# Attributes and places carried in the factors' PSUM banks, the head's order, and VectorE's small steps, in a PaiNN block on one core

## Chip, core and metric

The kernel runs on one core of a Trainium2 chip. The metric is the device time of one execution in microseconds (us); the kernel before was run three times. Besides, one execution was taken by the hardware profiler; its page and its trace are what is read below.

Engines go by the profile's names: PE is TensorE (matrix products and transposes; PEld is its loading of weights), DVE is VectorE, ACT is ScalarE, POOL is GpSimd, SP is SyncE. PSUM is the memory into which PE writes: banks of 512 float32 columns on each of 128 lanes.

## What is computed

One message block of a graph network (PaiNN) with a residual and a layer norm, over 1250 nodes of 512 numbers (384 are three components of a vector of 128, by c and k; 128 are scalars `s`) and 40000 edges, sorted by destination. Cut to what matters here:

```python
x_j = x[src]                                   # 40000 x 512
v_j, s_j = x_j[:, :384].reshape(E, 128, 3), x_j[:, 384:]
s_j = silu(s_j @ W1 + b1) @ W3 + b3
rbf = sqrt(2 / R_CUT) * sin(n * pi * r / R_CUT) / r     # n = 1..20
edge_basis = rbf * cutoff(r) @ W2 + b2                  # 40000 x 384
s1, s2, s3 = split(s_j * edge_basis)
v_msg = v_j * s1[:, :, None] + s3[:, :, None] * edge_attr[:, None, :]
x = x + segment_sum(concat(v_msg, s2), dst)
# a second block on x: node products with U, V, Wu1, Wu2, gathered
# by src again and summed by dst; then layernorm(x_in + x)
```

## The kernel before

**Head.** The node part `silu(s W1 + b1) W3 + b3` is computed once a node, multiplied into the node's vectors, and stored as ten blocks of 128 rows of `table1` in DRAM (`make_rows`, `table_row`). Its inputs arrive over three DMA queues: SP's (`w1`, `b1`, `b3`, `w3`, destinations, sources, weights, later the attributes and the weights of the second part), ACT's and POOL's (node rows). `keep_warm(12)` lets PE multiply ones until there is work. Destinations (`dst_r`) become places in a window of 32 nodes (`local_r`, L346); two reductions and a product (L378) count the edges that miss their window, and a branch on that count picks the windowed form, the only one that runs here. `part_bias` splits bias rows into two half-precision parts, once for the first part's columns (DVE) and once for the second's (POOL). `by_tile` turns sources, weights and places so that an edge is a lane.

**Batches.** The edges are 20 groups of four chunks of 512. One batch takes 128 edges of each of the four chunks of a group, so there are 80 batches, t = 4g + i with i = 0 to 3. For batch t:

- `gather(t)` (L756, POOL): four indirect DMAs bring 128 rows of `table1` each, three batches ahead. The first of the four is made to wait for `edge_factors` of the batch that PE has just made.
- `edge_factors(t)` (L906, PE): four products of the turned basis (21 rows) with W2 and b2 give 384 columns of factors in each of the four banks of `eb`. Columns 384 to 511 of these banks are not used.
- `messages(t)` (DVE): L916 and L918 multiply the gathered rows by the factors, in place; then what is listed under `amid`; then for batch t (`make_pair`, L939) and for batch t + 1 (`make_hot`, L847, `make_spread`, L859) the one-hot matrices of the edges' places, the latter two out of `sh.local` and `sh.attr`, which are parts of `sh.carried` (places and three attributes for each edge) in SBUF.
- `add_messages(t - 1)` (L955, L961, PE) sums the messages of the batch before into `agg` by the one-hot matrices.
- `count_links(t - 1)` (L976 at a group's first batch, L984; PE) counts weighted links between nodes into the bank `adj`, for the second block. It uses 400 columns of `adj`. The rest hold a table of halves (L802) and, copied on ACT every fourth group by `bring_fades` (L809), the fades of four groups, which DVE reads in `make_basis` and `make_turns`.
- `distances(t + 1)` (L871) and `mark_sources(t + 1)` (L881) make the one-hot matrices of sources on ACT, four operations each.

Every other group needs a new basis: `make_turns` in four parts (three on DVE, part 3 is a sine on ACT), `make_basis` for each of two groups (L814, DVE), and `turn_basis` (four transposes on PE, L823, and a copy on ACT, L828). At the end of a group, `close_group` on ACT copies the sums (L1000, L1006) and, in `close_links` (L1019 to L1024), the counts' high parts; `low_counts` (L1030, DVE) makes the low parts. For each block of 128 nodes the second part's node work follows on all engines (L1046 and on, L1092 among it).

**The order** is written out by hand. The main loop goes over t; in each step come `messages(t)`, the list `first`, `add_messages(t - 1)`, `count_links(t - 1)`, the list `early`, `edge_factors(t + 1)`, `gather(t + 3)`, and the lists `mid`, `late` and `dve`. Each list is sorted by rank. Every engine has a queue of its own and works in this order; waits between engines follow from the data. In a step that has something under `amid`, except a group's first, `count_links` comes behind `edge_factors` and `gather`:

```python
behind = set(amid) - {last + 1 for last in last_step.values()}
...
    if 1 <= t <= NT:
        add_messages(t - 1)
        if t not in behind:
            count_links(t - 1)
    run(early, t)
    if t + 1 < NT - 2:
        made = edge_factors(t + 1)
    ...
    if t in behind:
        count_links(t - 1)
```

For g > 1 with an odd number (base = 4g - 4) `amid` holds `make_turns` part 0 in t = base - 3, `make_basis(g)` in base + 2 and `make_basis(g + 1)` in base + 4; and for every group `low_counts` in the second step of the group after. `turn_basis` is in `first` of base + 3 and in `early` of base + 5, rank 1. `mark_sources` has rank 5 in `early`.

## Time and profile before

| | |
|---|---|
| three runs, median (lowest, highest) | 571.47 us (568.67, 572.39) |
| the profiled execution, its own time | 567.24 us |
| its span in the profile | 565.4 us |
| mean granted clock of PE | 0.907 of full |
| busy: PE, DVE, ACT, POOL | 79%, 76%, 67%, 62% |
| indirect DMAs, software queue | 104.47 MB, 62.6% of 16 engines' span |

How to read the lines: in a timeline, a row is start in us, duration in us, engine, line of the kernel, operation, the tile written <- the tiles read, their shape and the number of instructions it groups, and in brackets the idle time of the engine before it with what ended that idle time. In the waits, a row is the waiting engine, tile and line <- what released it: microseconds of idle time, number of waits, the longest. On the page, a group's row ends with busy time and mean nanoseconds of one, then the idle time ahead of them and its main releaser. "issue" is idle time for which the profile shows no cause.

### The profile page before, as it was taken

How to read it: one execution, taken by the hardware profiler on the slowest of the kernel's cores; microseconds unless marked ns; L12 is line 12 of the kernel's file. 1: busy time of each engine (PE TensorE's matmuls, PEld its weight loads, DVE VectorE, ACT ScalarE, POOL GpSimd, SP SyncE). 2: the span in 40 equal slices, each digit the busy share in tenths (PEclk: the TensorE clock that was granted, in tenths of full speed). 3: DMA queues.
4: the chain of work that ended last, by engine and by line, in shares of the span. 5: the costliest groups of instructions: out<-in, count | busy, mean ns of one | idle time of the engine just before them, and what ended most of it. 6: DMA issues, size and time to landing. Idle time of an engine off the chain costs nothing.

```text
span 565.4 us, 11226 instructions
## 1 busy us (share of the span) xinstructions
PE 444.6 (79%) x4257; PEld 249.3 (44%) x4257; DVE 432.1 (76%) x660; ACT 377.0 (67%) x955; POOL 350.1 (62%) x377
## 2 busy tenths in 40 slices
PE   8557667677878787767887797879789698989993
PEld 6323233353344344435433443545445354445682
DVE  5576687778877877886778778787878887797675
ACT  3493565567777566775757687577768766788663
POOL 7775666666666666665556665666666666574530
PEclk9856998979897979988788897999989999999997
DMA  8786777777777776776777787678778777877413
GB/s 247 269 243 188 227 228 221 226 214 227 234 222 203 239 223 214 228 230 192 209 217 217 205 258 231 193 234 250 220 237 229 236 224 223 265 217 237 157 56 133
DMA packets 37938, 123.29 MB, mean 218 GB/s; under 512 B 7296, under 2 KB 9870, under 8 KB 37874
## 3 DMA queue, kind: packets, MB, share of 16 engines
q0 software_dynamic: 25824, 104.47, 62.6%
q1 hardware_dynamic: 10850, 17.35, 9.3%
q8 instruction: 35, 0.57, 0.4%
q10 hardware_dynamic: 1200, 0.66, 0.4%
q14 instruction: 29, 0.24, 0.2%
HBM read 112.94 MB, written 9.51 MB: 217 GB/s over the span
## 4 chain that ended last, share of the span: by engine, by line
PE 55%; DVE 20%; ACT 13%; issue 6%; another core or an unknown queue 3%; DMA 2%; POOL 0%; SPq 0%; DVEq 0%; POOLq 0%
PE eb L906 11%; PE agg L955 8%; PE agg L961 6%; DVE more L918 5%; PE adj L984 5%; PE begun L1359 5%; ACT one L881 5%; DVE nodes L918 4%; DVE more L916 3%; PE work L1146 3%; DVE nodes L916 3%; PE work L1051 2%; PE work L823 2%; ACT one L871 2%
## 5 line engine op out<-in xcount | busy, mean ns | idle before, releaser
L756 POOL DMA_INDIRECT more<-table,src_i x189 | 188.8, 999 | 106.2 <-issue 43.0
L756 POOL DMA_INDIRECT nodes<-table,src_i x124 | 123.5, 996 | 68.4 <-issue 28.6
L881 ACT ACTIVATE one<-one,weight,src_f 128x128 f16<-128x128 f16 x313 | 128.6, 483 | 0.2
L916 DVE TENSOR_TENSOR more<-more,eb 128x1024 f32<-128x1024 f32 (+2 forms) x48 | 57.2, 1193 | 63.8 <-PE eb L906 29.9
L871 ACT ACTIVATE one<-number,low 128x128 f16<-128x128 f16 x313 | 99.8, 393 | 6.9 <-remote 4.6
L906 PE MATMUL eb<-w_sb,basis_t 21*128 21x384 f32 x614 | 78.9, 577 | 29.4 <-DVE more L918 14.5
L918 DVE TENSOR_TENSOR more<-more,eb 128x1536 f32<-128x1536 f32 (+2 forms) x48 | 81.8, 1705 | 0.0
L916 DVE TENSOR_TENSOR nodes<-nodes,eb 128x1024 f32<-128x1024 f32 x30 | 36.6, 1222 | 39.4 <-PE eb L906 21.3
L955 PE MATMUL agg<-more,hot 128*32 128x512 f32 x378 | 61.7, 687 | 5.2 <-ACT sums L1006 5.2
L961 PEld LDWEIGHTS agg<-more,spread 128*32 128x32 f32 x1134 | 39.6, 119 | 37.8 <-issue 36.6
L984 PE MATMUL adj<-pair,one 128*128 128x160 f16 x313 | 38.0, 243 | 22.6 <-DVE basis L814 18.7
L918 DVE TENSOR_TENSOR nodes<-nodes,eb 128x1536 f32<-128x1536 f32 x30 | 52.4, 1747 | 0.0
L961 PE MATMUL agg<-more,spread 128*32 128x128 f32 x1134 | 48.6, 291 | 2.7 <-issue 2.7
L906 PEld LDWEIGHTS eb<-w_sb,basis_t 21*128 21x128 f32 x614 | 26.5, 198 | 51.9 <-issue 22.8
L859 DVE TENSOR_TENSOR spread<-hot,carried 128x384 f32<-128x384 f32 (+1 forms) x81 | 44.4, 549 | 2.7
L955 PE MATMUL agg<-nodes,hot 128*32 128x512 f32 x248 | 40.6, 658 | 3.9 <-ACT sums L1006 3.8
L984 PEld LDWEIGHTS <-one 128*128 128x128 f16 x313 | 23.4, 103 | 38.3 <-issue 36.4
L939 DVE TENSOR_TENSOR pair<-number,column 128x640 f16<-128x640 f16 (+1 forms) x81 | 38.7, 479 | 0.0
L961 PEld LDWEIGHTS agg<-nodes,spread 128*32 128x32 f32 x744 | 25.5, 118 | 23.1 <-issue 22.7
L961 PE MATMUL agg<-nodes,spread 128*32 128x128 f32 x744 | 31.8, 289 | 1.0 <-issue 0.9
L828 ACT COPY basis_t<-work 128x512 f32<-128x512 f32 x20 | 11.7, 587 | 29.6 <-PE adj L984 12.3
L1359 PE MATMUL begun<-upper,cast 128*128 128x512 f32 x57 | 28.1, 493 | 0.2 <-ACT cast L1350 0.2
(289 smaller groups left out, 711.2 us busy)
## 6 DMA issues: line engine op xcount, KB each, us to landing
table<-more SPq DMA_DIRECT2D x10, 320.0 KB
more<-table,src_i POOLq DMA_INDIRECT x189
spilled<-begun SPq DMA_DIRECT2D x10, 256.0 KB
more<-spilled SPq DMA_DIRECT2D x2, 1280.0 KB
node_x<-in_x_dram SPq DMA_DIRECT2D x35, 64.0 KB
nodes<-table,src_i POOLq DMA_INDIRECT x124
out_dram<-more SPq DMA_DIRECT2D x7, 256.0 KB
nodes<-in_x_dram POOLq DMA_DIRECT2D x2, 768.0 KB
```

The lines of the kernel that those rows point to most:

```text
L756: got = nc.gpsimd.indirect_dma_start(out=rows_t[:n, j, :], out_offset=None, in_=sh.table1, in_offset=bass.IndirectOffsetOnAxis(ap=sh.src_i ...
L859: nc.vector.tensor_mul(spread[t][:m, js], hots[t][:m, js, None, :].to_broadcast(shape), sh.attr[:m, g, e : e + n, :, None].to_broadcast(sh ...
L871: nc.scalar.activation(onehots[t][:, j, :], number[:, :P], AF.Abs, bias=low[:, e : e + 1])
L881: nc.scalar.activation(one, one, AF.Relu, scale=less[:, e : e + 1], bias=worth[:, e : e + 1])
L906: made = nc.tensor.matmul(made_in[t][:, j, :V], turned[g][rows, i, :], sh.w2_sb[rows, :], start=True, stop=True,)
L916: nc.vector.tensor_mul(msg[:m, js, V:], msg[:m, js, V:], factors_of(t, js)[:m, :, C:V])
L918: nc.vector.tensor_mul(msg[:m, js, :V].rearrange("p t (k c) -> p t k c", k=3), msg[:m, js, :V].rearrange("p t (k c) -> p t k c", k=3), fac ...
L939: nc.vector.tensor_tensor(pair[:m, js, :].rearrange("p t (l h) -> p t l h", h=2), number[:m, : PARTS * WIN].rearrange("p (l h) -> p l h", ...
L955: nc.tensor.matmul(agg[j * WIN : (j + 1) * WIN, :], hots[t][:, j, :], msg[:, j, :width], start=(i == 0), stop=False, skip_group_check=True,)
L961: nc.tensor.matmul(agg[j * WIN : (j + 1) * WIN, c * C : (c + 1) * C], spread[t][:, j, c, :], msg[:, j, width:], start=False, stop=(i == la ...
L984: nc.tensor.matmul(to[:, :, at : at + WIN], one[:m, j, :], pair[:m, j, :].rearrange("e (p n) -> e p n", n=WIN), start=(i == 0 and j == js[ ...
L1359: nc.tensor.matmul(acc, casts[a, b], rows[:, a, :], start=(start and a == first and k == 0), stop=(stop and a == end - 1 and k == 1),)
```

## The change

- **Carried columns.** A new step `bring_carried(g)`, for g = 1 to 18, copies the places and attributes of a group (16 tiles of 4 numbers, 64 columns) on ACT from `sh.carried` into columns 384 to 447 of bank 0 or 1 of `eb` (by g mod 2), in `early` of t = 4g - 3 at rank 6.5. `make_hot` and `make_spread` of those groups read them there.
- **The list `amid` is gone.** `low_counts` is at the end (`dve`) of a group's closing step t = 4g + 4; `make_turns` part 0 at the end of base - 3, part 3 at the end of base + 1; `make_basis(g)` and `make_basis(g + 1)` at the ends of base + 2 and base + 3. `count_links` is ahead of `edge_factors` in every step.
- **Head.** Half as many warming products; `w3` second on SP's queue; destinations ahead of the outer node rows there; fills of `dst_r` on DVE, of `src_r` later on POOL; the addition of MARGIN to the sources on DVE in place of POOL; the second bias rows and their `part_bias` earlier; three blocks of rows instead of one ahead of the product that counts the misses; eight loads of w2 and b2 from POOL's queue to SP's, behind the attributes.

```diff
--- before.py
+++ after.py
@@ -154,6 +154,8 @@
         return t
 
 
+    inside = SHARE * (NCP - 1) - MARGIN
+    assert all(0 <= inside - (SHARE * c - MARGIN) < WIN for c in range(full, NCP))
     ones = const.tile([P, P], F32)
     nc.vector.memset(ones, 1.0)
     warm = const.tile([P, 1], F32, name="warm")
@@ -164,23 +166,20 @@
         for _ in range(n):
             nc.tensor.matmul(idle[:, :P], ones, ones, start=True, stop=True)
 
-    keep_warm(12)
+    keep_warm(6)
     bias_f = front.tile([BIAS_ROWS - 1 + 32, V + 2 * C], F32, name="bias_f")
     nc.vector.memset(bias_f, 0.0)
+    dst_r = front.tile([NCP, CHUNK], I32, name="dst_r")
+    nc.vector.memset(dst_r[unfilled:, :], inside)
     sh.nodes = const.tile([P, NB * width], F32, name="nodes")
     sh.xt = sh.nodes.rearrange("p (b f) -> p b f", f=width)
     last = n_nodes + MARGIN - (NB - 1) * P
     nc.vector.memset(sh.xt[last // 32 * 32 :, NB - 1, :], 0.0)
     nc.vector.memset(sh.xt[:MARGIN, 0, :], 0.0)
 
-    inside = SHARE * (NCP - 1) - MARGIN
-    assert all(0 <= inside - (SHARE * c - MARGIN) < WIN for c in range(full, NCP))
-    dst_r = front.tile([NCP, CHUNK], I32, name="dst_r")
-    nc.gpsimd.memset(dst_r[unfilled:, :], inside)
     diff = front.tile([P, P], I32)
     nc.gpsimd.iota(diff, pattern=[[1, P]], base=0, channel_multiplier=-1)
     part = numbers([P, 1], [[0, 1]], 0, 1, "part")
-    nc.gpsimd.memset(sh.src_r[unfilled:, :], 0.0)
 
     size = CPG * (V + 2 * C)
     sh.more = const.tile([P, 3 * size], F32, name="more")
@@ -199,18 +198,19 @@
     of_s = slice(V, width)
     load_inner(nc.scalar, of_s, 1)
     sh.w1_sb = load(nc.sync, w1, [C, C], "w1_sb")
+    sh.w3_sb = load(nc.sync, w3, [C, V], "w3_sb")
     load_inner(nc.scalar, of_s, 5)
     nc.scalar.activation(warm, warm, AF.Silu)
     for b0 in (1, 5):
         load_inner(nc.gpsimd, slice(0, V), b0)
+    nc.gpsimd.memset(sh.src_r[unfilled:, :], 0.0)
     load_outer(nc.gpsimd, slice(0, V))
     sh.b1_sb = load(nc.sync, b1.rearrange("(p o) -> p o", o=1), [C, 1], "b1_sb")
     first_last = slice(0, 3, 2)
     three = bias_f.rearrange("(r q) f -> r q f", q=32)[:, 0, :]
     nc.sync.dma_start(three[:, :V], b3.rearrange("(o f) -> o f", o=1).to_broadcast([3, V]))
-    sh.w3_sb = load(nc.sync, w3, [C, V], "w3_sb")
+    load_edges(dst_r, dst)
     load_outer(nc.sync, of_s)
-    load_edges(dst_r, dst)
     load_edges(sh.src_r.bitcast(I32), src)
 
 
@@ -344,12 +344,6 @@
 
     local_r = front.tile([NCP, CHUNK], F32)
     nc.gpsimd.tensor_scalar(local_r, dst_r, share, None, op0=ALU.subtract)
-    nc.gpsimd.tensor_scalar(sh.src_r, sh.src_r.bitcast(I32), float(MARGIN), None, op0=ALU.add)
-    for i in range(GROUP):
-        nc.gpsimd.dma_start(w2_sb[i * FEAT : i * FEAT + N_RBF, :], w2)
-        nc.gpsimd.dma_start(
-            w2_sb[i * FEAT + N_RBF : i * FEAT + N_RBF + 1, :], b2.rearrange("(o f) -> o f", o=1)
-        )
     ends = front.tile([NCP, 2], F32)
     misses = front.tile([NCP, 1], F32)
     missed_i = fields.tile([1, 1], I32)
@@ -358,8 +352,15 @@
     make_rows((1, 2))
     inner_layer(next_s, (5, 6, 7, 8))
     load_edges(sh.wgt_r, edge_weight)
+    for h in range(2):
+        nc.sync.dma_start(
+            three[:, V + h * C : V + (h + 1) * C],
+            bu2.rearrange("(h o c) -> h o c", o=1, c=C)[2 * h].to_broadcast([3, C]),
+        )
+    part_bias(nc.gpsimd, slice(V, V + 2 * C))
     make_rows((3, 4))
     nc.vector.tensor_reduce(ends[:, 0:1], local_r, AX.X, ALU.min)
+    nc.vector.tensor_scalar(sh.src_r, sh.src_r.bitcast(I32), float(MARGIN), None, op0=ALU.add)
     rest_s = turn_s((0, 9))
     make_rows((5,))
     nc.vector.tensor_reduce(ends[:, 1:2], local_r, AX.X, ALU.max)
@@ -369,22 +370,20 @@
     nc.vector.scalar_tensor_tensor(
         misses, ends[:, 0:1], 0.0, ends[:, 1:2], op0=ALU.is_lt, op1=ALU.max
     )
-    for h in range(2):
-        nc.sync.dma_start(
-            three[:, V + h * C : V + (h + 1) * C],
-            bu2.rearrange("(h o c) -> h o c", o=1, c=C)[2 * h].to_broadcast([3, C]),
-        )
-    make_rows((7,))
+    make_rows((7, 8, 0))
     nc.tensor.matmul(missed, misses, ones[:NCP, 0:1], start=True, stop=True)
-    make_rows((8,))
     nc.vector.tensor_copy(missed_i, missed)
-    make_rows((0, 9))
+    make_rows((9,))
     by_tile(ps_front, sh.src_r, 0, 1, sh.src_f, 1)
     by_tile(ps_front, sh.wgt_r, 0, 1, sh.weight, 1)
     by_tile(ps_front, local_r, 0, 1, sh.local, 1)
     nc.vector.tensor_copy(sh.src_i, sh.src_f)
-    part_bias(nc.gpsimd, slice(V, V + 2 * C))
     load_edges(sh.att_r, edge_attr, 3)
+    for i in range(GROUP):
+        nc.sync.dma_start(w2_sb[i * FEAT : i * FEAT + N_RBF, :], w2)
+        nc.sync.dma_start(
+            w2_sb[i * FEAT + N_RBF : i * FEAT + N_RBF + 1, :], b2.rearrange("(o f) -> o f", o=1)
+        )
     sh.u_sb = load(nc.sync, u, [C, C], "u_sb")
     sh.v_sb = load(nc.sync, v, [C, C], "v_sb")
     sh.wu1_sb = load(nc.sync, wu1.rearrange("(h p) f -> p h f", p=C), [C, 2, C], "wu1_sb")
@@ -834,6 +833,18 @@
                 if m < P:
                     engine.memset(tile[m:, j], 0.0)
 
+        carried_at = {}
+
+        def bring_carried(g):
+
+            to = eb[:, g % 2, V : V + EPG * CARRY].rearrange("p (t k) -> p t k", k=CARRY)
+            nc.scalar.copy(to, sh.carried[:, g])
+            carried_at[g] = to
+
+        def carried_of(g):
+
+            return carried_at.get(g, sh.carried[:, g])
+
         def make_hot(t):
 
             g, i = batches[t]
@@ -847,7 +858,7 @@
                 nc.vector.tensor_tensor(
                     hots[t][:m, js, :],
                     lane[:m, None, :WIN].to_broadcast(shape),
-                    sh.local[:m, g, e : e + n, None].to_broadcast(shape),
+                    carried_of(g)[:m, e : e + n, 3:].to_broadcast(shape),
                     op=ALU.is_equal,
                 )
 
@@ -859,7 +870,7 @@
                 nc.vector.tensor_mul(
                     spread[t][:m, js],
                     hots[t][:m, js, None, :].to_broadcast(shape),
-                    sh.attr[:m, g, e : e + n, :, None].to_broadcast(shape),
+                    carried_of(g)[:m, e : e + n, :3, None].to_broadcast(shape),
                 )
 
         def distances(t):
@@ -920,7 +931,6 @@
                     msg[:m, js, :V].rearrange("p t (k c) -> p t k c", k=3),
                     factors_of(t, js)[:m, :, None, :C].to_broadcast([m, n, 3, C]),
                 )
-            run(amid, t)
             make_pair(t)
             if t == 0:
                 make_spread(0)
@@ -1448,7 +1458,7 @@
             last_step[g] = t
 
 
-        first, early, late, dve, mid, amid = {}, {}, {}, {}, {}, {}
+        first, early, late, dve, mid = {}, {}, {}, {}, {}
 
         def at(when, step, rank, fn, *args):
             when.setdefault(step, []).append((rank, fn, args))
@@ -1459,10 +1469,7 @@
             if g == NGR - 1:
                 at(dve, end - 4, 9, clear_unused, g)
                 at(early, end, 0.3, close_links, g)
-            if end + 1 < NT:
-                at(amid, end + 1, 1, low_counts, g)
-            else:
-                at(dve, end, 5, low_counts, g)
+            at(dve, end, 5, low_counts, g)
         for t in range(NT):
             if t + 1 < NT:
                 at(first, t, 9, distances, t + 1)
@@ -1470,17 +1477,14 @@
 
         for g in range(1, NGR, 2):
             base, n = 4 * g - 4, min(2, NGR - g)
-            if base:
-                at(amid, base - 3, 4, make_turns, g, n, 0)
-            else:
-                at(dve, 0, 4, make_turns, g, n, 0)
+            at(dve, max(0, base - 3), 4, make_turns, g, n, 0)
             at(dve, max(0, base - 2), 5, make_turns, g, n, 1)
             at(dve, base - 1 if base else 1, 6, make_turns, g, n, 2)
-            at(*((early, base + 1, 5.5) if base else (dve, 1, 7)), make_turns, g, n, 3)
-            at(amid, base + 2, 5, make_basis, g)
+            at(dve, base + 1, 7, make_turns, g, n, 3)
+            at(dve, base + 2, 5, make_basis, g)
             at(first, base + 3, 1, turn_basis, g)
             if n > 1:
-                at(amid, base + 4, 4, make_basis, g + 1)
+                at(dve, base + 3, 4, make_basis, g + 1)
                 at(early, base + 5, 1, turn_basis, g + 1)
 
 
@@ -1690,6 +1694,8 @@
         bring_fades(1)
         for g in range(1 + FADES, NGR, FADES):
             at(early, 4 * g - 3, 6, bring_fades, g)
+        for g in range(1, NGR - 1):
+            at(early, 4 * g - 3, 6.5, bring_carried, g)
         distances(0)
         mark_sources(0)
         ahead = 3
@@ -1697,7 +1703,6 @@
             gather(t)
         gather(ahead - 1, edge_factors(0))
         make_hot(0)
-        behind = set(amid) - {last + 1 for last in last_step.values()}
         for t in range(max(*first, *early, *late, *dve, *mid) + 1):
             if t < NT:
                 messages(t)
@@ -1710,8 +1715,7 @@
             run(first, t)
             if 1 <= t <= NT:
                 add_messages(t - 1)
-                if t not in behind:
-                    count_links(t - 1)
+                count_links(t - 1)
             run(early, t)
             if t + 1 < NT - 2:
                 made = edge_factors(t + 1)
@@ -1719,8 +1723,6 @@
                 edge_factors(t + 2)
             if t + ahead < NT:
                 gather(t + ahead, made if t + ahead < NT - 2 else None)
-            if t in behind:
-                count_links(t - 1)
             run(mid, t)
             run(late, t)
             run(dve, t)
```

## Prediction

> **What bounds the kernel now.** I read the page first. No engine is full over the span: PE 79%, VectorE (DVE) 76%, GpSimd (POOL) 62%, so the limit lies in a loop between engines.
>
> ```profile
> span 565.4 us, 11226 instructions
> PE 444.6 (79%) x4257; PEld 249.3 (44%) x4257; DVE 432.1 (76%) x660; ACT 377.0 (67%) x955; POOL 350.1 (62%) x377
> ...
> L756 POOL DMA_INDIRECT more<-table,src_i x189 | 188.8, 999 | 106.2 <-issue 43.0
> L756 POOL DMA_INDIRECT nodes<-table,src_i x124 | 123.5, 996 | 68.4 <-issue 28.6
> ```
>
> Next I read the timeline of one batch. It is t = 37, a batch with t mod 8 = 5 (t counts the 80 batches; t = 4g + i).
>
> ```profile
> 270.44 1.22 DVE L916 TENSOR_TENSOR more<-more,eb 128x1024 f32<-128x1024 f32 x1 [2.77 <-PE eb L906]
> 270.68 0.96 POOL L756 DMA_INDIRECT nodes<-table,src_i  x1 [2.17 <-PE eb L906]
> ...
> 271.58 1.75 DVE L918 TENSOR_TENSOR more<-more,eb 128x1536 f32<-128x1536 f32 x1
> ...
> 272.81 0.66 PE L823 MATMUL work<-ident,basis 128*128 128x128 f32 x4
> ...
> 273.39 0.93 PE L906 MATMUL eb<-w_sb,basis_t 21*128 21x384 f32 x8
> ...
> 274.47 1.22 POOL L756 DMA_INDIRECT nodes<-table,src_i  x1 [0.30 <-issue]
> ...
> 275.09 0.56 DVE L859 TENSOR_TENSOR spread<-hot,carried 128x384 f32<-128x384 f32 x1
> 276.43 0.59 ACT L828 COPY basis_t<-work 128x512 f32<-128x512 f32 x1 [3.14 <-PE adj L984]
> 276.52 1.22 DVE L916 TENSOR_TENSOR nodes<-nodes,eb 128x1024 f32<-128x1024 f32 x1 [0.87 <-PE adj L984]
> ...
> 276.91 1.65 ACT L881 ACTIVATE one<-one,weight,src_f 128x128 f16<-128x128 f16 x4
> ```
>
> Two things are to be seen. L906 starts 0.06 us after L918 ends (273.33) and is over at 274.32, yet L916 of the next batch begins only at 276.52. L823 is over at 273.47, and the scalar engine (ACT), idle for 3.14 us, takes its result only at 276.43. PE's results are seen by the others all at once, some 0.7 us after the end of the batch's fourth gather (274.47 + 1.22 = 275.69). In the last batches no gather runs, and the same product is seen 0.10 us after its end (519.95 + 0.92 = 520.87, then 520.97):
>
> ```profile
> 519.95 0.92 PE L906 MATMUL halves<-w_sb,basis_t 21*128 21x384 f32 x4 [0.18 <-DVE more L918]
> ...
> 520.97 0.68 DVE L916 TENSOR_TENSOR nodes<-nodes,halves 128x512 f32<-128x512 f32 x1
> ```
>
> So a batch is a loop: the signal of the factors releases L916 and the first gather (270.44, 270.68), four gathers follow, and then the next signal comes, 276.52 - 270.44 = 6.1 us later. I call the moment at which PE's results are seen "the late signal". It lies 3.2 us after L918's end. Whatever PE, ACT and DVE finish before it is hidden; what comes after it lengthens the batch.
>
> Last I read the waits between engines.
>
> ```profile
> PE adj L984 <- DVE basis L814: 18.7, 9, 2.7
> ...
> PEld adj L976 <- ACT adj L809: 10.0, 4, 3.2
> ...
> PE adj L976 <- ACT adj L809: 7.3, 4, 2.5
> ```
>
> These are the key to the change. L809 copies the fades into columns from 420 on of the bank `adj`; L976 writes columns below 400 of it, and waits for that copy in all four batches in which there is one. L814 reads the same spare columns, and L984 waits for it in nine batches. So a product waits for every earlier copy into, and read from, its bank, though the columns are others.
>
> **The change, part by part.** (A) *The copy `bring_carried`* is on ACT, in the early list at rank 6.5 of batch t = 4g - 3, g = 1 to 18, behind `mark_sources` (L881) and ahead of `edge_factors(t + 1)` (L906). It writes into a bank that L906 then writes, so by the waits above L906 must wait for it. In a batch with t mod 8 = 5, ACT's queue ahead of it is L828, which is released only by the late signal, and L881. From the rows: L828 at 276.43, L881 ends at 276.91 + 1.65 = 278.56. The copy has 64 columns a lane as L809 has, 0.20 us (row below): 278.76. L906 takes 0.93: 279.7. L916 starts then at 279.75 instead of 276.52, which is 3.2 us. The first gather of the next batch waits for the same product, so nothing of it is made up later. Nine batches (5, 13, ... 69): 9 x 3.2 = +29. Bounds: if L823's result reached ACT at once, with the links' 0.45 us (L984, ahead of L823 now) before it, L828 would start at 273.9, L881 end at 276.2, and the product at 277.35: 0.9 a batch, +8; if L881 is pushed too, 3.6, +32. I take 29, because L828 waited 3.14 here and the gathers stay as they are.
>
> (B) *Low counts ahead of the products*, with the copy of the batch after. `low_counts` (L1030) moves from behind the products of batch 4k + 1 to the end of batch 4k, where it needs L1024 of the same batch. This is t = 32 and 33:
>
> ```profile
> 242.86 1.22 DVE L916 TENSOR_TENSOR nodes<-nodes,eb 128x1024 f32<-128x1024 f32 x1 [1.40 <-PE work L1051]
> ...
> 243.46 0.56 ACT L1024 ACTIVATE counts<-high,shifts 128x320 f16<-128x320 f32 x1
> ...
> 245.66 0.48 DVE L1030 SCALAR_TENSOR_TENSOR counts<-counts,adj 128x320 f16<-128x320 f16 x1
> ...
> 247.37 1.63 ACT L881 ACTIVATE one<-one,weight,src_f 128x128 f16<-128x128 f16 x4
> ...
> 248.98 1.22 DVE L916 TENSOR_TENSOR nodes<-nodes,eb 128x1024 f32<-128x1024 f32 x1 [0.40 <-remote]
> 249.54 0.20 ACT L809 COPY adj<-fade 128x64 f32<-128x64 f32 x1
> 249.79 0.72 PE L976 MATMUL adj<-passed,ident 128*128 128x80 f32 x2 [2.54 <-ACT adj L809]
> ```
>
> L1024 ends at 244.02, L1030 would end at 244.5, and L916 of t = 33 starts there instead of at 242.86: 1.7 us. Behind it stand all of VectorE's products, and the pair, hot and spread of the next batch. Then L881 ends at 249.0, the fades (0.20) and the carried columns (0.20) follow, L906 ends at 250.35 and L916 of t = 34 starts at 250.4 instead of 248.98. The two delays overlap, so the pair of batches loses 1.4; another 0.4 if ACT's copy L1000, which came before the late signal here, comes with it. I take 1.6 for eight pairs (t mod 8 = 0 and 1): +13; bounds 0.8 (the copy finds its room) and 2.4: +6 to +19. At t mod 8 = 4 the same move is hidden by (A), at no cost; without that cover, about 0.9 in five batches.
>
> (C) *Waits that go.* With turns and basis at a batch's end, `count_links` stands ahead of L906 in every batch and neither L984 nor L976 waits for DVE or ACT there: 18.7 + 7.3 = 26 us of PE's idle time. Of this only what made L906 later than the late signal was on the path; a wait of 2 us is hidden by the 3.2. The worst case is the one above, 2.54 us at 249.79. I take a third: -8, bounds 0 and -26. The moved basis (L814) now needs L984's signal of its own batch and so follows the late signal by its 0.4; the next batch's loop (below) has 0.85 to spare, so it costs nothing; without that room, 18 x 0.4 = 7.
>
> (D) *Hot and spread read PSUM.* L906 then waits for the spread too. Pair, hot and spread take 0.40 + 0.32 + 0.56 = 1.3 behind L918 (274.37 to 275.65), so L906 runs from 1.3 to 2.3 instead of from 0.06 to 1.0 after L918. The late signal at 3.2 hides that: L916 to L918's end 2.9, 1.3, 0.93 and latencies are 5.2 of 6.1 us. Without this cover it is 1.3 for each of some 70 batches. The operations themselves: no row has a hot or a spread that reads PSUM. The nearest is L1092, as wide as a hot (128 columns) and with `work`, a PSUM bank, as an input: 0.28 against 0.29 of L847, which reads SBUF alone. I take 0 for both.
>
> ```profile
> 246.46 0.29 DVE L847 TENSOR_TENSOR hot<-lane,carried 128x128 f32<-128x128 f32 x1
> ...
> 247.83 0.28 DVE L1092 TENSOR_TENSOR x<-node_x,work 128x128 f32<-128x128 f32 x1
> ```
>
> The gathers may gain: 0.96 us is the undisturbed one (270.68), the mean of 313 is 0.998, together 12 us. I take nothing, as the signal in t = 37 came no later behind a gather of 1.22 than in other batches; bounds 0 and -12. The Trainium skill (GPSIMD Engine Reference, Key points) says that GpSimd shares its SBUF interfaces with VectorE and contends with its instructions of two SBUF inputs; hot and spread stop being such, while pair stays one. The stretched gather beside the spread at 274.47 agrees; by that page alone the sum would be up to 12 us less.
>
> (E) *Head.* Destinations load ahead of the outer rows, and the misses' product goes behind three more rows:
>
> ```profile
> 14.74 1.57 POOL L346 TENSOR_SCALAR local_r<-dst_r,share 80x512 f32<-80x512 int32 x1 [2.97 <-DMA dst_r<-in_dst_dram]
> ...
> 19.06 0.19 PE L378 MATMUL missed<-ones,misses 80*1 80x1 f32 x2 [2.07 <-DVE misses L369]
> ```
>
> PE's stop of 2.07 goes; adding MARGIN leaves POOL. Half of the warming products go as well. The w2 and b2 loads, eight issues, move past the attributes on SP's queue; they are needed only by the first L906. I take -2.5, bounds -4 and +1.
>
> Sum: 29 + 13 - 8 + 0 - 2.5 = +31.5. Against the profiled execution (567.24, span 565.4) that is 598.7. The three runs' median, 571.47, lies 4.2 above it, so the forecast of the median is 603.
>
> **Rivals.** *R1, the signal comes early:* PE's lateness belongs to the order in which L823 and L906 stand, not to the gathers, and ACT gets L823 at once. For it: L828's waits differ from batch to batch; against it: ACT idle at 276.43 with L823 done. Then (A) is +8: 571.5 + 8 + 13 - 8 - 2.5 = 582. *R2, the product is not held, and the kernel gets faster:* the factors' bank is guarded by columns. Then (A) is 0; in (B) the loop 2.9 + 0.1 + 0.93 has 2.1 to spare, more than 1.7, so 0; (C) and (E) stay: 571.5 - 10.5 = 561. It decides where L906 at t mod 8 = 5 starts within 0.1 us of L918's end. Against it: the four of four waits of L976 for L809. With the 12 us of the gathers it would be 549. *R3, it does not do what it says:* losses and gains of (B), (C) and (E) cancel and (A) is hidden, because ACT is ahead in the longer batches: 571.5 + 13 - 8 - 2.5 - 3 = 571. Against it: the late signal, not ACT's load, holds L828.
>
> **How the numbers follow.** Forecast 0.52, R1 0.18, R2 0.20, R3 0.10. R2 gets the most of the three, as its one condition, how the bank is guarded, decides the largest term, and the trace shows the guard only in another bank (`adj`). The likeliest is 603, with its own range 590 to 616 from the bounds of (A), (B) and (C). The range to be given reaches from 566, half way between R3 and R2, so that it leaves out R2 alone, to 616: 0.8. A measurement tells about 1% (5.7 us) from no change: slower 0.52 + 0.18 = 0.70, same 0.10, faster 0.20.
>
> **What would show it.** Right: in batches 5, 13, ... 69, L906 waits for the new copy, and the time from L916 to L916 is about 9.3 us instead of 6.1; in batches 1 mod 8, L916 waits for low counts; L984's wait for the basis is gone; the other batches stay at 6.0 to 6.1. Wrong: L906 starting at L918's end, no wait of PE for ACT's copy, or a batch of less than 6.0 us, which would mean that the late signal is not what sets the loop.

## The result and the profile after

The changed kernel takes 630.24 us (median of four runs, 629.89 to 631.30) against 571.93 us (four runs, 568.67 to 573.67) for the kernel before: ratio 1.103, 95% interval 1.098 to 1.108. The forecast was 603 with a range up to 616. The sign and the place of the largest loss were right, the size was not: 58 us were lost where 31.5 were forecast. Of the five terms of the sum only one, (A), came near what was measured.

The page after, its first lines and the groups of the gathers and of the factors' product (the product has line 917 now, the first multiplication of a batch 927, the copy of the carried columns 841):

```profile
span 628.5 us, 11273 instructions
PE 471.7 (75%) x4245; PEld 260.4 (41%) x4245; DVE 433.8 (69%) x662; ACT 378.2 (60%) x973; POOL 330.3 (53%) x367
...
L755 POOL DMA_INDIRECT more<-table,src_i x189 | 181.1, 958 | 152.6 <-PE eb L917 84.4
L755 POOL DMA_INDIRECT nodes<-table,src_i x124 | 117.9, 951 | 97.7 <-PE eb L917 54.1
L917 PE MATMUL eb<-w_sb,basis_t 21*128 21x384 f32 x614 | 83.5, 601 | 101.7 <-ACT eb L841 39.8
```

DVE and ACT are busy as long as before. POOL's gathers are shorter, 951 and 958 ns in place of 996 and 999, but its idle time ahead of them rose from 174.6 to 250.3 us (106.2 + 68.4 and 152.6 + 97.7), and its releaser is now the factors' product, which itself stood idle for 101.7 us, 39.8 of them for the new copy. PE is 27 us busier (471.7 against 444.6) with 12 instructions fewer: the same products run longer.

The batch t = 37 after (rows of the timeline: start, duration, what ended the idle time):

```profile
297.53 0.94 POOL L755 DMA_INDIRECT nodes<-table,src_i  x1 [0.30 <-issue]
297.54 1.21 DVE L927 TENSOR_TENSOR more<-more,eb 128x1024 f32<-128x1024 f32 x1
298.67 1.75 DVE L929 TENSOR_TENSOR more<-more,eb 128x1536 f32<-128x1536 f32 x1
...
299.10 1.94 PE L965 MATMUL agg<-more,hot 128*32 128x512 f32 x8
...
302.95 0.60 PE L822 MATMUL work<-ident,basis 128*128 128x128 f32 x4
...
303.59 0.59 ACT L827 COPY basis_t<-work 128x512 f32<-128x512 f32 x1 [2.35 <-PE work L822]
304.07 1.65 ACT L892 ACTIVATE one<-one,weight,src_f 128x128 f16<-128x128 f16 x4
305.62 0.20 ACT L841 COPY eb<-carried 128x64 f32<-128x64 f32 x1
...
305.88 1.61 PE L917 MATMUL eb<-w_sb,basis_t 21*128 21x384 f32 x8 [2.33 <-ACT eb L841]
...
307.77 0.94 POOL L755 DMA_INDIRECT more<-table,src_i  x1 [6.79 <-PE eb L917]
307.94 1.22 DVE L927 TENSOR_TENSOR nodes<-nodes,eb 128x1024 f32<-128x1024 f32 x1 [3.97 <-PE eb L917]
```

This is the chain that the prediction drew: turned basis, `mark_sources`, copy, product, and only then the next batch, 307.94 - 297.54 = 10.4 us after the last. One link differs: ACT takes the transposes (L822) as soon as they end, but they end late. Two of its durations are new: the product takes 1.61 in place of 0.93, and the sums L965 1.94 in place of 1.06 (both from t = 37 before).

Where the time went, by batch. The table adds, over the batches with the same t mod 8, the time from the start of one batch's first VectorE product (L916 or L927) to the next one's; it is worked out from the timelines. The columns are the profiled executions of five kernels, four of which are told of below.

| t mod 8 | before | after | c_early | no_carried | low_alone |
|---|---|---|---|---|---|
| 0 | 60.5 | 76.9 | 75.9 | 71.8 | 75.9 |
| 1 | 64.2 | 63.5 | 61.9 | 57.8 | 56.2 |
| 2 | 63.7 | 69.4 | 69.5 | 60.6 | 54.6 |
| 3 | 64.3 | 65.2 | 64.4 | 66.3 | 67.3 |
| 4 | 61.8 | 69.0 | 69.5 | 64.9 | 66.7 |
| 5 | 57.5 | 89.5 | 65.9 | 63.2 | 52.8 |
| 6 | 59.8 | 57.3 | 57.1 | 57.2 | 57.9 |
| 7 | 54.5 | 55.2 | 55.2 | 55.3 | 54.4 |

After against before: +32.0 in 5 mod 8, +16.4 in 0, +7.2 in 4, +5.7 in 2. Batches 2 and 4 mod 8, which were to stay at 6.0 to 6.1 us, take about 7.

### The profile page after: what moved, and what is told of

It is laid out like the page before. It is cut to its first block, busy times and chain, and to the rows that moved or that the text cites. A ratio compares the mean times of both kernels' runs of the same rounds, so it can differ in the third digit from the quotient of the medians.

```text
span 628.5 us, 11273 instructions
## 1 busy us (share of the span) xinstructions
PE 471.7 (75%) x4245; PEld 260.4 (41%) x4245; DVE 433.8 (69%) x662; ACT 378.2 (60%) x973; POOL 330.3 (53%) x367
## 4 chain that ended last, share of the span: by engine, by line
PE 53%; DVE 19%; ACT 16%; issue 7%; DMA 0%; another core or an unknown queue 0%; DVEq 0%; ACTq 0%
PE eb L917 15%; PE agg L965 10%; ACT one L892 6%; PE agg L971 6%; DVE more L929 5%; PE work L1156 3%; DVE more L927 3%; PE begun L1369 3%; DVE nodes L929 3%; PE adj L994 3%; DVE nodes L927 2%; ACT one L882 2%; PE work L1140 2%; DVE pair L949 2%; PE work L822 1%
## 5 line engine op out<-in xcount | busy, mean ns | idle before, releaser
L755 POOL DMA_INDIRECT more<-table,src_i x189 | 181.1, 958 | 152.6 <-PE eb L917 84.4
L755 POOL DMA_INDIRECT nodes<-table,src_i x124 | 117.9, 951 | 97.7 <-PE eb L917 54.1
L917 PE MATMUL eb<-w_sb,basis_t 21*128 21x384 f32 x614 | 83.5, 601 | 101.7 <-ACT eb L841 39.8
L927 DVE TENSOR_TENSOR more<-more,eb 128x1024 f32<-128x1024 f32 (+2 forms) x48 | 57.0, 1190 | 53.7 <-PE eb L917 36.3
L917 PEld LDWEIGHTS eb<-w_sb,basis_t 21*128 21x128 f32 x614 | 27.3, 200 | 125.1 <-ACT eb L841 43.9
L965 PE MATMUL agg<-more,hot 128*32 128x512 f32 x378 | 71.6, 821 | 2.5 <-ACT counts L1034 1.9
L971 PEld LDWEIGHTS agg<-more,spread 128*32 128x32 f32 x1134 | 44.1, 137 | 44.5 <-issue 42.7
L971 PE MATMUL agg<-more,spread 128*32 128x128 f32 x1134 | 52.7, 326 | 0.0
L927 DVE TENSOR_TENSOR nodes<-nodes,eb 128x1024 f32<-128x1024 f32 x30 | 36.5, 1217 | 23.0 <-PE eb L917 16.0
L1040 DVE SCALAR_TENSOR_TENSOR counts<-counts,adj 128x320 f16<-128x320 f16 x20 | 9.7, 487 | 47.7 <-ACT counts L1034 31.2
L965 PE MATMUL agg<-nodes,hot 128*32 128x512 f32 x248 | 40.7, 711 | 2.5 <-ACT sums L1016 1.3
L870 DVE TENSOR_TENSOR spread<-hot,eb 128x384 f32<-128x384 f32 x72 | 39.9, 554 | 2.5
L994 PE MATMUL adj<-pair,one 128*128 128x160 f16 x313 | 39.6, 253 | 1.0 <-issue 1.0
L949 DVE TENSOR_TENSOR pair<-number,column 128x640 f16<-128x640 f16 (+1 forms) x81 | 38.6, 477 | 0.0
L971 PEld LDWEIGHTS agg<-nodes,spread 128*32 128x32 f32 x744 | 27.1, 127 | 23.9 <-issue 23.4
```

Of the source, the lines that this page charges most:

```text
L755: got = nc.gpsimd.indirect_dma_start(out=rows_t[:n, j, :], out_offset=None, in_=sh.table1, in_offset=bass.IndirectOffsetOnAxis(ap=sh.src_i ...
L870: nc.vector.tensor_mul(spread[t][:m, js], hots[t][:m, js, None, :].to_broadcast(shape), carried_of(g)[:m, e : e + n, :3, None].to_broadcas ...
L917: made = nc.tensor.matmul(made_in[t][:, j, :V], turned[g][rows, i, :], sh.w2_sb[rows, :], start=True, stop=True,)
L927: nc.vector.tensor_mul(msg[:m, js, V:], msg[:m, js, V:], factors_of(t, js)[:m, :, C:V])
L949: nc.vector.tensor_tensor(pair[:m, js, :].rearrange("p t (l h) -> p t l h", h=2), number[:m, : PARTS * WIN].rearrange("p (l h) -> p l h", ...
L965: nc.tensor.matmul(agg[j * WIN : (j + 1) * WIN, :], hots[t][:, j, :], msg[:, j, :width], start=(i == 0), stop=False, skip_group_check=True,)
```

## The experiments

Runs told of together share a chip, and runs of the kernel before on it. They fell on five chips of two kinds: two on which the kernel before takes 567 to 573 us, as in the record above, and three on which it takes 494 to 496. Each run is therefore compared with the kernel before on its own chip, and times are subtracted only within one kind.

**The carried columns: alone, with the copy early, without, and in SBUF.** These four ran on one chip (before: 573.10 us). `c_alone` is the kernel before with the new step and the new reads of `make_hot` and `make_spread`. `c_early` is the changed kernel with one number changed:

```diff
-            at(early, 4 * g - 3, 6.5, bring_carried, g)
+            at(early, 4 * g - 3, 0.5, bring_carried, g)
```

`no_carried` leaves out the two lines that schedule the step, so that `carried_of` gives SBUF for every group. `sbuf_copy` keeps copy and rank, with another destination:

```diff
-            to = eb[:, g % 2, V : V + EPG * CARRY].rearrange("p (t k) -> p t k", k=CARRY)
+            to = pool.tile([P, EPG, CARRY], F32, name="brought", bufs=2)
```

> The kernel before with bring_carried alone (copy at rank 6.5, hot and spread read the factors' banks); nothing else of the change. Theory (the copy stands behind ACT's late work and holds the next product, since a product waits for an earlier copy into its bank): the nine batches with t mod 8 = 5 take about 9.3 us in place of 6.1, +29 to +32 in all, so 601 to 604 us. Rival (the loss of these batches comes from the other moves, low counts, turns and basis, and the copy only shows as the last releaser): below 580 us, batches 5 mod 8 at 6.1 to 6.8 us. If the shorter gathers (951 and 958 ns after, 996 and 999 before) come from hot and spread leaving SBUF, they are 950 to 960 ns here too.

> The changed kernel with the copy's rank 0.5 in place of 6.5: the same copy in the same batch, but on ACT ahead of the basis' copy and of mark_sources. Theory (it is the place in ACT's queue): batches 5 mod 8 fall from 9.9 us to 6.1 to 6.6, so 598 to 602 us. Rival (the product is held by hot and spread, which read its banks, whatever the copy does): L917 still waits, batches 5 mod 8 above 8 us, 620 us or more.

> The changed kernel without bring_carried: hot and spread read SBUF as before; all the other moves stay. Theory: batches 5 mod 8 at 6.1 us, -32 against the changed kernel: 596 to 600 us; gathers back at 996 to 999 ns mean. Second theory (reads of the factors' banks by hot and spread cost more, because they hold every product for 1.3 us): below 594 us, and below c_early by more than 4 us. Rival (the carried columns cost little): above 615 us.

> The changed kernel with the same copy at the same rank into an SBUF tile of its own, which hot and spread read. ACT does the same work in the same place; only the bank is not written and not read. Theory (the wait is on the bank): no product waits for this copy, batches 5 mod 8 at 6.1 to 6.6 us, 596 to 602 us. Rival (ACT's added work and its order are the cost, or hot waits for the late copy): batches 5 mod 8 above 8 us, 620 us or more.

Measured: `c_alone` 625.88 us (ratio 1.092, 1.084 to 1.100), `c_early` 602.95 (1.054, 1.046 to 1.062), `no_carried` 584.92 (1.022, 1.015 to 1.030), `sbuf_copy` 582.62 (1.015, 1.007 to 1.023). The columns alone cost 53 us, not 29 to 32; by the table's working 38.6 of them lie in batches 5 mod 8 and 14.7 in batches 1 mod 8, the two that have a copy. With the columns in, all other parts of the change add some 4 us. Moving the copy takes 27.3 us off the changed kernel; taking the columns away another 18.0; 11.8 are left. (The changed kernel's 630.24 is from the chip of the section above, where the kernel before takes 1.2 us less, so the 4 and the 27.3 are good to a us or two.) `sbuf_copy` does ACT's work in ACT's place without the bank and costs nothing beside `no_carried`, so the place in the factors' banks is the cost and not ACT's time. The theory of `c_early` (the place in ACT's queue, 598 to 602) came within 1 us. The first theory of `no_carried` (596 to 600) and that of `sbuf_copy` (596 to 602) missed by 11 us and more, since neither counted the reads. The second theory of `no_carried` (reads that hold the product) holds: 584.92 is below 594, and 18.0 below `c_early`.

The gathers did not follow their forecast: they take 964 and 966 ns in `c_alone`, but 972 and 959 in `no_carried`, where hot and spread read SBUF as before, and not 996 to 999. So what made them shorter is not only that hot and spread left SBUF, and stays open.

How the reads hold it: the waits of the product in `c_early` and in `no_carried` (waiting engine, tile, line <- releaser: us, times, longest).

```profile
PE eb L917 <- DVE spread L870: 23.5, 16, 2.4
...
PE eb L917 <- DVE hot L858: 11.2, 9, 1.6
PE eb L917 <- ACT eb L841: 10.8, 7, 1.9
```

```profile
PE eb L917 <- DVE more L929: 18.7, 14, 6.0
...
PE eb L917 <- DVE nodes L929: 11.1, 11, 2.2
```

What it costs is seen in t = 33, a batch behind a long one. First `no_carried`:

```profile
253.62 1.21 DVE L927 TENSOR_TENSOR nodes<-nodes,eb 128x1024 f32<-128x1024 f32 x1
...
256.81 0.93 PE L917 MATMUL eb<-w_sb,basis_t 21*128 21x384 f32 x8
...
258.49 1.26 POOL L755 DMA_INDIRECT more<-table,src_i  x1 [1.53 <-DVE x L1102]
...
258.85 1.21 DVE L927 TENSOR_TENSOR nodes<-nodes,eb 128x1024 f32<-128x1024 f32 x1
```

then `c_early`:

```profile
259.28 1.21 DVE L927 TENSOR_TENSOR nodes<-nodes,eb 128x1024 f32<-128x1024 f32 x1
...
262.79 0.55 DVE L870 TENSOR_TENSOR spread<-hot,eb 128x384 f32<-128x384 f32 x1
...
263.43 0.22 ACT L841 COPY eb<-carried 128x64 f32<-128x64 f32 x1 [1.14 <-DVE spread L870]
...
263.70 1.62 PE L917 MATMUL eb<-w_sb,basis_t 21*128 21x384 f32 x8 [1.83 <-ACT eb L841]
...
265.43 1.22 DVE L927 TENSOR_TENSOR nodes<-nodes,eb 128x1024 f32<-128x1024 f32 x1 [0.85 <-ACT adj L808]
265.61 0.94 POOL L755 DMA_INDIRECT more<-table,src_i  x1 [3.42 <-PE eb L917]
```

In `no_carried` the product starts 3.19 us after L927, and the batch takes 5.23. In `c_early` the copy waits for the spread, which reads its tile, and the product for the copy; it starts 4.42 us after L927, runs at the lower rate, and the first gather waits 3.42 us for it. The batch takes 6.15.

**The other three parts alone.** On one chip (before: 567.11 us, 25 runs), each on the kernel before. `low_alone`:

```diff
-            if end + 1 < NT:
-                at(amid, end + 1, 1, low_counts, g)
-            else:
-                at(dve, end, 5, low_counts, g)
+            at(dve, end, 5, low_counts, g)
```

`turns_alone` has the change's lines for `make_turns` and `make_basis` and nothing else of it; `head_alone` all lines of the change ahead of `windowed`; `before_again` is the kernel before, for its trace.

> The kernel before with low counts moved to the end of a group's last step, nothing else. Theory: batches 0 mod 8 take about 1.6 us more and batches 4 mod 8 0.5, those behind them somewhat less: 6 to 13 us more than before. Rival (what is lost in batches 0 mod 8 comes back in 1 mod 8, where low counts no longer stand ahead of pair, hot and spread): within 3 us of before.

> The kernel before with the turns and the basis moved to the ends of batches, nothing else. Theory (the links no longer wait for the basis, and hot and spread come earlier): 0 to 8 us less than before; on a chip with 495 us rather more, 5 to 15 us less, since low counts and copy made basis_back 17 us slower than the changed kernel there. Rival (keep_rest behind a basis that waits for PE): 3 to 8 us more, in batches 2 and 3 mod 8.

> The kernel before with the changed head, nothing else. Theory (w3 and the destinations ahead in SP's queue make the bias rows, and with them the table, late): the first product of the factors starts 0.9 us later or more, the first gather 1.4 us later or more; 1 to 6 us more than before. Rival (the forecast): 1 to 4 us less, first gather before 27.5 us.

> The kernel before unaltered, for its trace on this chip. Where it takes 570 to 575 us: batches at 6.0 to 6.1 us as in the trace of the forecast. Where it takes 490 to 500 us: theory (there PE's signals are seen at once, so the batch is set by DVE, ACT and the products and no longer by the fourth gather): L916 starts within 0.2 us of L906's end, or right behind DVE's own work, and most batches take 4.5 to 5.1 us. Rival (the gathers are quicker there): gathers at under 0.9 us each.

Measured: `low_alone` 567.51 us (0.999, 0.995 to 1.003), `turns_alone` 570.67 (1.003, 0.999 to 1.008), `head_alone` 569.00 (1.000, 0.996 to 1.004), `before_again` 565.82. None of the three can be told from no change. The theory of `low_alone` (6 to 13 us more) was too large, that of `turns_alone` (a gain) had the wrong sign, and that of `head_alone` (1 to 6 us more) is not borne out by the time, though its late start is: the first gather starts at 29.77 us, against 27.96 in `before_again` on the same chip. The rival was right for `low_alone`: the table has +15.4 in batches 0 mod 8, as forecast, and -8.0 and -9.1 in the two behind. Its timeline at t = 32 and 33:

```profile
235.38 1.22 DVE L916 TENSOR_TENSOR more<-more,eb 128x1024 f32<-128x1024 f32 x1 [1.14 <-remote]
...
238.32 0.93 PE L906 MATMUL eb<-w_sb,basis_t 21*128 21x384 f32 x8 [2.00 <-DVE more L918]
...
241.64 0.96 POOL L756 DMA_INDIRECT more<-table,src_i  x1 [1.28 <-PE work L1051]
242.00 0.56 ACT L1024 ACTIVATE counts<-high,shifts 128x320 f16<-128x320 f32 x1
...
242.59 0.49 DVE L1030 SCALAR_TENSOR_TENSOR counts<-counts,adj 128x320 f16<-128x320 f16 x1 [2.61 <-PE work L1051]
242.90 0.95 POOL L756 DMA_INDIRECT more<-table,src_i  x1 [0.30 <-issue]
243.00 1.21 DVE L916 TENSOR_TENSOR nodes<-nodes,eb 128x1024 f32<-128x1024 f32 x1
...
248.25 1.22 DVE L916 TENSOR_TENSOR nodes<-nodes,eb 128x1024 f32<-128x1024 f32 x1
```

DVE waits for ACT's counts (L1024, done at 242.56) and starts L916 1.6 us late, but the product was done, so POOL's first gather starts 1.36 us ahead of L916 (241.64 and 243.00) in place of 0.24 behind it. Its four gathers are over earlier, and the next batch takes 5.25 us. `turns_alone` was to gain; its batch 2 mod 8 shows why not (t = 34):

```profile
256.02 0.93 PE L906 MATMUL eb<-w_sb,basis_t 21*128 21x384 f32 x8
257.80 0.49 DVE L814 TENSOR_TENSOR basis<-turn,adj 128x320 f32<-128x320 f32 x1 [1.99 <-PE eb L906]
...
258.21 0.68 DVE L1097 TENSOR_TENSOR h_t<-x,node_x 128x512 f32<-128x512 f32 x1
...
258.81 1.21 DVE L916 TENSOR_TENSOR more<-more,eb 128x1024 f32<-128x1024 f32 x1
```

The basis waits for PE's late signal as L916 would, and with `keep_rest` (L1097) behind it L916 comes a microsecond later. `make_turns` part 0, which reads `adj` too, now waits for the links at the end of batches 5 mod 8 (15.2 us in five waits on L984 over the run), a wait that the prediction had not priced. Batches 5 mod 8 take 77.6 us there against 57.5, and batches 4 and 6 mod 8 give those 20 us back.

**The copy without the reads, and `c_early` again.** `copy_only` is `c_alone` with `carried_of` returning `sh.carried[:, g]`: the copy is made and nobody reads it. Before took 495.09 us there.

> The kernel before with the copy bring_carried at rank 6.5, whose columns nobody reads: hot and spread read SBUF. Theory (the late copy alone holds the product in batches 5 and 1 mod 8): where the kernel before takes 565 to 575 us, batches 5 mod 8 at 9 to 10 us and 25 to 35 us more than before; 1 mod 8 longer by half of what c_alone showed (+14.7 in all). Rival (the wait is for the reading of the columns, not for the copy): no product waits for the copy, less than 5 us more.

> Here the kernel is c_early once more (all moves, copy early), beside copy_only on the same chip. Where the kernel before takes 565 to 575 us: 597 to 605 us, as before (603 against 573); where it takes 490 to 500 us: theory (the reading holds every product until the spread's end, batches at 5.12 us) 505 to 515 us, less than the changed kernel's 521.6.

Measured: `copy_only` 520.52 us (1.051, 1.046 to 1.056), `c_early` under its second label 499.95 (1.011, 1.005 to 1.017), below the 505 to 515 that were expected. The chip was of the other kind, so the size in batches 5 mod 8 for the first kind was not tried. The late copy alone costs 25 us, without any reader; 17 products wait for it, 37.6 us in all. The theory holds in that the copy alone holds the product, and the rival falls. ACT is late there without any late signal (t = 37):

```profile
241.14 0.66 PE L823 MATMUL work<-ident,basis 128*128 128x128 f32 x4
...
241.84 0.58 ACT L828 COPY basis_t<-work 128x512 f32<-128x512 f32 x1 [0.21 <-PE work L823]
...
244.13 0.94 PE L918 MATMUL eb<-w_sb,basis_t 21*128 21x384 f32 x8 [2.33 <-ACT eb L842]
```

ACT takes the transposes 0.04 us after their end (241.14 + 0.66). Its own queue, the copy of the basis and `mark_sources`, is enough to hold the product for 2.33 us.

**The parts undone one by one, on the quick chips.** `low_back` and `basis_back` put low counts, or turns and basis, back into the middle of a batch in the changed kernel (with `count_links` behind the product there); `w3_back` issues w3 behind b3; `c_early_alone` is `c_alone` with rank 0.5; `after_again` is the changed kernel unaltered. The first four ran on a chip with 494.21 us before, the later ones on another with 495.81.

> The changed kernel with the load of w3 back behind b3 on SP's queue; the rest of the head stays changed. Theory (w3, 196 KB, ahead of b1 and b3 delays the row b3, so the bias rows and the first rows of the table come 3.4 us later): the first wait for b3 (2.96 us) is gone, the first L927 starts at 37 us or earlier in place of 40.5, -3 to -4 us: 626 to 627. Rival (eight loads of w2 and b2 on SP's queue, or the order at the first gathers, set the start): first L927 stays at 39 us or later, 629 to 631.

> The changed kernel with low_counts alone back in the middle of the batch after (and count_links behind the product in those batches, as before). Theory (low counts at a batch's end hold VectorE until ACT's counts are ready): batches 0 mod 8 fall from 8.2 to 6.1 us, and batches 4 mod 8 from 7.0 to 6.2; the batches after (1 and 5) are not longer: 630 - 17 - 7 = 606 us, 604 to 615 with some given back in batches 5. Rival (these batches wait for ACT and PE anyway, low counts only shows it): 622 us or more.

> The changed kernel with turns and basis back where they were (in the middle of a batch, count_links behind the product there); low counts, copy and head stay changed. Theory (the basis at a batch's end waits for PE's late signal and has keep_rest behind it): batches 2 mod 8 fall from 7.0 to 6.2 us, 3 mod 8 a little: 622 to 625 us. Rival (PE's low clock after the long waits makes batches 2 mod 8 long, not the basis): no change, 629 to 632, batches 2 mod 8 still at 7.0. If the waits of the links on the basis (18.7 us before) were on the path, it is slower than 631.

> The kernel before with the copy at rank 0.5, hot and spread reading the factors' banks; nothing else of the change. Theory (the late signal after the fourth gather sets the batch, and the products held by hot and spread end before it): 568 to 573 us, batches at 6.0 to 6.1, whatever the gathers gain. Rival 1 (shorter gathers, 950 to 960 ns, shorten each batch by 4 x 0.04 us): 559 to 562 us. Rival 2 (hot and spread hold the product, 1.3 us a batch): 600 us or more.

> The changed kernel unaltered, as the reference of this chip for the three runs beside it. Where the kernel before takes 570 to 575 us, 628 to 632 us. On a chip like that of w3_back, where it takes 494 us and most batches take 5.12 us, the estimate is 518 to 522 us (w3_back's 518.3 and up to 4 us for the head).

> low_back again, beside the changed kernel on the same chip. Theory (low counts at a batch's end hold VectorE, batches 0 mod 8 at 8.2 us): 15 to 25 us less than the changed kernel where batches have the floor of 6.1 us. Rival (as on the other chip, where low_back took 10 us more than w3_back: low counts in the middle delay pair, hot and spread, which hold the product by its bank, so what is won in batches 0 mod 8 is lost in 5 mod 8): within 6 us of the changed kernel or slower.

> basis_back again, beside the changed kernel on the same chip. Theory (basis at a batch's end waits for PE's late signal): 5 to 8 us less than the changed kernel. Rival (turns and basis in the middle delay hot and spread, which hold the product, and the links wait for the basis; on the other chip it took 24 us more than w3_back): 5 to 25 us more.

Measured: `after_again` 521.61 us (1.054, 1.042 to 1.066), `w3_back` 518.26 (1.049, 1.039 to 1.060), `low_back` 528.43 and 526.25 (1.070 and 1.065), `basis_back` 542.12 and 538.33 (1.097 and 1.086), `c_early_alone` 528.67 (1.072, 1.063 to 1.082). `w3_back` is not told apart from the changed kernel, and nothing follows on the head. The others go against their theories: with the carried columns in place, putting turns and basis back costs 17 us there. What stands in the middle of a batch delays hot and spread, and these hold the product. On the quick chips the moves of VectorE's small steps are thus what makes the columns bearable; without the columns, on the slower chips where that was tried, they have nothing to give.

**Keeping PE busy in the wait.** Added work on the changed kernel, into columns that nobody reads:

```diff
+            if t % 8 == 5 and t < NT - 8:
+                for _ in range(20):
+                    nc.tensor.matmul(
+                        eb[:, CPG - 1, V:BANK], sh.ones, sh.ones, start=True, stop=True
+                    )
             if t + 1 < NT - 2:
                 made = edge_factors(t + 1)
```

> The changed kernel with 20 products of ones (128 x 128) on PE ahead of the held product in each batch with t mod 8 = 5, into unused columns of bank 3: added work whose result nobody reads. Theory (PE stands idle for some 5 us there, its clock is lowered, and the held product takes 1.66 in place of 0.93 us, the next sums 1.94 in place of 1.06): the product takes 0.93 us, batches 5 mod 8 are 0.6 to 0.8 us shorter and the batches behind them a little, so 5 to 9 us less than the changed kernel. Rival (the clock follows the average power or load, not this wait): the product stays at 1.66 us and the time is the same or longer.

It took 565.37 us (before 495.81, the changed kernel 521.61 on that chip) and missed its aim, for a reason worth more (t = 37, copy into bank 0):

```profile
274.75 0.20 ACT L841 COPY eb<-carried 128x64 f32<-128x64 f32 x1
...
275.00 6.36 PE L1722 MATMUL eb<-ones 128*128 128x128 f32 x40 [2.33 <-ACT eb L841]
...
281.29 0.93 PE L917 MATMUL eb<-w_sb,basis_t 21*128 21x384 f32 x8
```

The added products write bank 3, and they wait for the copy into bank 0. The hold is not on columns and not on a bank, but on the whole of `eb`, four banks in one tile. (In `c_early` at t = 33, too, the copy into bank 1 waited 1.14 us for a spread that reads bank 0.) So they could not fill the wait; they lengthened it. The product behind them took 0.93 in all nine such batches, but it does in seven of nine in `after_again` too, so the price of the clock was not measured by this run.

The Trainium skill (PSUM — Partial Sum Buffer, PSUM bank collisions raise a hardware error) asks for a guard by bank and quadrant, and finds accesses to different banks clean. The waits here are wider than that, as the row of L1722 shows. The row tells how this program is guarded, and not what the chip itself would need; banks in tiles of their own were not tried. No kernel of these runs is faster than the kernel before by more than its interval.

## Why the prediction was right and wrong, step by step

In the prediction's own terms: (A) was to cost 29 and gave some 27; (D) was to cost nothing and gave 18.0; (B), (C) and (E) together were to cost 2.5 and gave 11.8. The terms that failed are thus (D) above all, and then the sum of (B) and (C).

**(A), the copy: right in place and near in size, and partly by luck.** Forecast +29; moving the copy gave 27.3, and batches 5 mod 8 are 32.0 longer. The waits of the product for `bring_carried` are on the page. But the reason given, that ACT is released only by the late signal, holds in one of the nine batches after (t = 45, where ACT took the transposes 3.09 us after their end). In t = 5 and 29 it took them within 0.53 us, and these batches take 7.4 and 7.5 us. In the other six it took them within 0.04 us, but they ended 5.6 to 7.0 us into the batch, in place of 2.5 to 4.9 before. In t = 37 PE came to them late: the links now stand ahead of them, as the prediction had said, and PE ran slowly (L965, 1.94); what share belongs to which was not tried. In `c_alone`, where PE ran at full rate in this batch, ACT waited 2.29 us with the transposes done since 297.89, as forecast, and so it did in four of the nine batches there:

```profile
295.58 1.06 PE L967 MATMUL agg<-more,hot 128*32 128x512 f32 x8
...
297.23 0.66 PE L823 MATMUL work<-ident,basis 128*128 128x128 f32 x4
...
300.40 0.59 ACT L828 COPY basis_t<-work 128x512 f32<-128x512 f32 x1 [2.29 <-remote]
```

**(D), hot and spread: the step that failed most.** "The late signal at 3.2 hides that" holds for a batch in step: in `c_alone` each of the six sums without a copy (0, 2, 3, 4, 6 and 7 mod 8) is within 2.3 us of before. It does not hold for one behind a longer batch. There the gathers run ahead, and a batch of 5.2 us pays back what was lost, if the product starts at L918's end. Held until the spread, and the copy behind it, it cannot. 0 was taken, 18.0 us were measured. The early copy is in that figure, but in the table 17.6 us between `c_early` and `no_carried` lie in batches 0, 2 and 4 mod 8, which have no copy. The working had all the numbers for this (loop 5.2 against 6.1), but it treated 6.1 as fixed. Its own sign of being wrong, a batch of less than 6.0 us, came: 5.85 in t = 38 of the changed kernel, 5.25 in `low_alone`, 5.23 in `no_carried`.

**(B), low counts: failed in its sum.** The delay was sized well (15.4 in batches 0 mod 8 against 8 x 1.6 = 13), but alone it costs nothing, since two batches give it back. That "nothing of it is made up later" was argued for (A), where POOL waits too, and was carried silently to (B), where POOL does not. The prediction priced (B) together with the copy of the batch after, which `low_alone` leaves out. In the changed kernel, which has both, batches 0 and 1 mod 8 are 15.7 us longer, near the 13, and batches 2 mod 8 give nothing back: with the columns in, the product is held there too.

**(C), the waits that go: failed.** -8 was taken, +1.9 was measured with an interval from -0.5 to +4.3 (0.9992 to 1.0075 of 567). The failing step is that the next batch's loop "has 0.85 to spare, so it costs nothing": in batches 2 mod 8 `keep_rest` stands behind the basis.

**(E), the head: -2.5 was not reached.** Alone it is within 0.4% of nothing (-2.3 to +2.1 us). In the profiled executions the first L927 after starts at 40.51 and L916 before at 36.94; `head_alone` has 41.27 and `before_again` 37.12, on one chip. So the traces have the batches start some 4 us later where the forecast had them earlier, and the medians show no loss; where the 4 us come back was not found.

**What no step had: together.** The three parts without the columns cost 11.8 us (`no_carried`), alone the sum of their medians is 0.4 + 3.6 + 1.9 = 5.9, and of their ratios 1.2 (-0.6 + 1.9 - 0.1). By the table, batches 1, 2 and 5 mod 8 together, which give back in `low_alone` (56.2 + 54.6 + 52.8 = 163.6), give back less in `no_carried` (57.8 + 60.6 + 63.2 = 181.6), where basis and turns stand at the ends of batches 2, 3 and 5. That this is the cause is argued, not shown.

**What no step had: PE's rate.** A product that costs 0.93 takes 1.6 to 1.66 where PE had stood; in the trace after, all three products of the factors behind 3 us or more of idle PE did so, in `c_alone` six of ten. PE's busy time grew by 27 us, and the granted clock fell from 0.907 to 0.844. The Trainium skill (TensorE: Matmul & The Clock Gate, Part 1: The HAM clock gate) says that the array falls to half its rate after some 3.4 us without work. The rows agree in size (0.93 to 1.66), but the length of the stop alone does not tell: a product behind 2.33 us took 1.66 after, and one behind 3.52 us took 0.93 in `c_alone`. The lower rate is inside the 27.3 and 18.0 above and has no measured price of its own.

The rivals: R2 and R3 fall, since PE waits for the copy (R2) and the losses are not cancelled (R3). R1 falls by its number, as (A) is not +8; but its condition, that ACT gets the transposes at once, holds in most of the nine batches after.

## What to carry to other kernels

Free columns beside a product's output are not free: a copy into them, or a read from them, orders the whole tile against the next product, here four banks. Ask who writes the tile next, and what stands in that writer's queue. And a delay has to be followed for two more batches: where the engine that sets the pace (here the gathers) is not held too, the next batches give it back; where it is, little comes back. So price not the delay but whether the pacemaker waits.

## What the runs showed of the hardware

Chips differ by 14 to 16% on one and the same kernel: 567 and 573 us on two, 494 to 496 on three. The late signal is a matter of the chip, as far as the traces tell; none is of the kernel before on a quick one. A batch of `after_again`, on one of the three:

```profile
258.38 1.22 DVE L927 TENSOR_TENSOR nodes<-nodes,eb 128x1024 f32<-128x1024 f32 x1 [0.34 <-PE eb L917]
...
262.37 0.95 POOL L755 DMA_INDIRECT more<-table,src_i  x1 [0.30 <-issue]
...
262.51 0.93 PE L917 MATMUL eb<-w_sb,basis_t 21*128 21x384 f32 x8 [1.52 <-DVE spread L870]
...
263.51 1.22 DVE L927 TENSOR_TENSOR more<-more,eb 128x1024 f32<-128x1024 f32 x1 [0.26 <-PE eb L917]
```

The fourth gather runs as long as elsewhere (0.95), and the product is seen 0.07 us after its end (263.44). There the batch is the loop through the hold: L927 to the spread's end and the product, 5.13 us, which is the floor of most batches. In `copy_only`, where nobody reads the columns, batches 3 and 7 mod 8 take 4.8 us on average. Why PE's signals come late on the other two chips no run here could tell, and it stays open.
